# A two-layer graph network on Trainium2: which nodes of the output share a partition

## The chip, the cores and the metric

The kernel runs on one core of one Trainium2 chip. The metric is the device time of one execution in microseconds; the median of five runs of the kernel before is 2661.31 us. Five engines work side by side, each through its own list of instructions, and wait for one another by semaphores: TensorE (PE; its weight loads are listed apart as PEld), VectorE (DVE), ScalarE (ACT), GpSimd (POOL) and SyncE (SP). Data moves between the main memory (DRAM in the code) and the on-chip memory of 128 partitions through 16 DMA engines; SP and POOL put transfers on them, each through a queue of its own.

## What is computed

Sixteen graphs of N = 1024 nodes with C = 256 features go through two layers. All numbers are 32-bit floats. Cut to what matters:

```python
# layer 0: attention over the nodes, with a residual
h = relu(layernorm(x))
x = x + L0(h, para, adj, kv_w)
# layer 1: graph convolution and two linear layers, with a residual
h = relu(layernorm(x))
agg  = A_hat @ h                      # normalised adjacency, per graph
y1   = relu(batchnorm(agg @ W1.T + b1, g1, be1))    # 512 features
out  = batchnorm(y1 @ W2.T + b2, g2, be2)           # 256 features
x = x + out
```

The two batch norms take mean and variance over all nodes of all 16 graphs. So the second one can be applied only when the last graph's product with W2 is done, and the residual, the output of layer 0 (here x1), is needed again only then.

## The kernel before

P = 128 partitions, NT = N / P = 8 blocks of nodes, CC = C / P = 2 blocks of features, FB = 512.

**Layer 0 and the first half of layer 1** fill the span up to about 2380 us. `attention()` walks through the 16 graphs; the other products of the neighbouring graphs are woven between its steps by a hand-written order (`background`, `weave`, `advance`) in which every piece yields its cost in microseconds. Node t * 128 + p of a graph lies in partition p of the tile `xs[b]`, block t. When a graph's attention is complete, `normed` (for the last graph `normed_last`) puts the layer norm's output into a tile `h` and stores `xs[b]`, which is x1, from POOL's queue to `x1_d[b]` in DRAM (L725, L736). `x1_d[b]` has the shape [128, 8, 256], the same as the tile, so each partition's 8 KB are one contiguous run. POOL's queue also carries the stores of layer 1's hidden rows (`y_d`, L709), the sums of attention (`sums_d`, L919) and their return (`inv`, L924). SP's queue carries the loads.

**The second half of layer 1** is the generator `second`. For each graph `graph(b)` makes the product with W2, by seven partial products m1 to m7 (`product`, L1180), in a form that has features in partitions: `y2[b][k]` is a tile [128 features, 1024 nodes] for each block k of features. Between the graphs `load_x1` brings x1 of the graphs back from `x1_d` into tiles `xo` (L1111), two loads of 512 KB for each graph, one for each half of the blocks. The buffers of xo are borrowed from tiles that are no longer used: the first three graphs have a pool of their own, the next ones take buffers of `yin` and of `both`, graphs 8 to 10 the `y2` tiles of graphs 0 to 2, and later ones the buffers again that earlier xo leave.

**The tail** is the last loop of `second`, over the 16 graphs. `scales` and `affs` give the scale and shift of the second batch norm. For each graph:

1. ACT applies scale and shift to `y2[b][k]` in place (L1303), 1024 nodes in one instruction; for graph 0 in two parts of 512 nodes, so that the first transposes can begin sooner.
2. PE transposes blocks of 128 features x 128 nodes into PSUM, so that nodes are in partitions (L1311): four transposes (two node blocks, two feature blocks) make one tile `pt`. The pool `ps` has four such tiles.
3. DVE adds `pt` to the residual `xo` in place (L1317), two node blocks at a time.
4. After half a graph, which is two such sums, POOL stores 512 KB to `out` (L1318).
5. After the graph, `load_x1` is called if graphs remain to be loaded; SP waits there for the buffer.

The loop issues all instructions in this order; each engine runs its own list in order. A transposed block t holds the nodes t * 128 to t * 128 + 127, so that partition p gets node t * 128 + p:

```python
nc.tensor.transpose(
    pt[:, j, k * P : (k + 1) * P],
    y2[b][k][:, t * P : (t + 1) * P],
    ident,
)
```

In `out` a partition's four rows of a half graph lie 128 KB apart, and each row is 1 KB.

A second copy of the program (`layers(True)`) runs only if the attention's sums leave a safe range; with these inputs it doesn't.

Of the kernel before, what the change touches and what calls it, by code (L numbers as in the profile page):

```python
# [10 lines left out]
F32 = mybir.dt.float32  # L11
# [6 lines left out]
P = 128  # L18
# [5 lines left out]
def gnn_two_layers_kernel(  # L24
# [12 lines left out]
    nc = tc.nc  # L37
    B, N, C = x.shape
    H1 = w1_t.shape[1]
    NT = N // P  # L40
# [3 lines left out]
    FB = 512  # L44
# [8 lines left out]
    dram = ctx.enter_context(tc.tile_pool(name="dram", bufs=1, space=DRAM))  # L53
# [9 lines left out]
    stats1 = const.tile([P, HC, B * NH, 6], F32, name="stats1")  # L63
    mv1 = const.tile([P, HC, 2], F32, name="mv1")

    x1_d = [dram.tile([P, NT, C], F32, name=f"x1_d{b}") for b in range(B)]


    aht_d = dram.tile([7, NP // 2, P, TH, FB], F32, name="aht_d")
# [14 lines left out]
    def layers(shifted):  # L84
# [23 lines left out]
        xs, hs, hts, ats, qs, ks, vs = {}, {}, {}, {}, {}, {}, {}  # L108
# [19 lines left out]
        def run(*parts):  # L128
            for part in parts:
                while advance(part) is not None:  # L130
                    pass
            while queue:
                queue.pop(0)()

        def weave(main, *sides):

            for i, cost in enumerate(main):
                for start, side in sides:
                    if i >= start:
                        cost += next(side, 0.0)  # L140
                yield cost
            for _, side in sides:
                yield from side
# [16 lines left out]
        def load_x(b):  # L160
            xs[b] = p3.tile([P, NT, C], F32, tag="x", name=f"x_{b}")
            for half in range(2):
                t = slice(half * NT // 2, (half + 1) * NT // 2)
                nc.sync.dma_start(
                    out=xs[b][:, t], in_=x[b].rearrange("(t p) c -> p t c", p=P)[:, t]
                )

        def load_adj(q, th, name):
            t = p3.tile([P, TH, FB], F32, tag="adj", name=name)
            nc.sync.dma_start(  # L170
                out=t,
                in_=adj[th * TH * P : (th + 1) * TH * P, q * FB : (q + 1) * FB].rearrange(
                    "(t p) m -> p t m", p=P
                ),
            )
            return t

        load_x(0)
        kvw = const.tile([P, CC, 2 * C], F32, tag="kvw", name=f"kvw_{kind}")
        nc.sync.dma_start(out=kvw, in_=kv_w.rearrange("(k p) j -> p k j", p=P))  # L180
        rows = big.tile([P, NH, NT], F32, name="rows")

        def columns_of(col, name):

            cbs = []
            for g in range(NT // 4):
                cb = py.tile([P, 4, P], F32, tag="y", name=f"cb_{name}_{g}")
                nc.vector.tensor_copy(
                    cb, col[:, 4 * g : 4 * g + 4].unsqueeze(2).to_broadcast([P, 4, P])
                )  # L190
                cbs.append(cb)
            return cbs
# [191 lines left out]
        def differences(b, cbs):  # L384

            cbcs[b] = p1.tile([P, N], F32, tag="cbc", name=f"cbc_{b}")
            broadcast_row(cbcs[b], cbs, f"c{b}")
            weighers[b] = weigh(b)
# [332 lines left out]
        def normed(b):  # L721
            while (b, NH - 1) not in complete:
                yield 0.1
            yield from Norm(b, False).all()
            nc.gpsimd.dma_start(out=x1_d[b], in_=xs[b])  # L725
            if b + 3 < B:
                load_x(b + 3)

        def normed_last():

            norm = Norm(B - 1, False)
            for half in range(NH):
                while (B - 1, half) not in complete:
                    yield 0.0
                yield from norm.half(half * NT // 2)
            nc.gpsimd.dma_start(out=x1_d[B - 1], in_=xs[B - 1])  # L736

        def prepare(b, products):

# [270 lines left out]
        with st:  # L1010
            if shifted:
                for b in range(B):
                    if b > 0:
                        load_x(b)
                    run(Norm(b, True).all())
                    differences(b, columns_of(csums[b], f"c{b}"))
                    for k in range(CC):
                        transposed(b, k)
                    run(islice(weighers[b], AHEAD))
                    run(weave(plain_queries(b), (0, weighers[b])))  # L1020
                    if b == 0:
                        run(degrees(), graph())
                        load_later()
                        broadcast_row(later["dbc"], columns_of(dinv, "deg"), "deg")
                    run(keys_values(b))
                    shifted_attention(b)
                    norm = Norm(b, False)
                    run(norm.all())
                    nc.gpsimd.dma_start(out=x1_d[b], in_=xs[b])
                    if b == B - 1:  # L1030
                        attn.close()
                        turns.append(second(kind))
                    run(aggregate(b), hidden(b))
            else:
                norm = Norm(0, True)
                norm.stats(0, 1)
                norm.scale(0, 2)
                for t in range(2, NT, 2):
                    norm.stats(t, t + 1)
                    norm.shift(t - 2, 2)  # L1040
                    norm.relu(t - 2, t - 1)
                    norm.scale(t, 2)
                norm.shift(NT - 2, 2)
                norm.relu(NT - 2, NT - 1)
                products = keys_values(0)

                for k in range(CC):
                    transposed(0, k, (0,))
                run(islice(products, 2))
                for k in range(CC):  # L1050
                    transposed(0, k, (1,))
                differences(0, columns_of(csums[0], "c0"))
                run(weave(products, (0, islice(weighers[0], AHEAD))))
                load_x(1)
                load_x(2)
                run(weave(plain_queries(0), (0, weighers[0]), (5, Norm(1, True).all())))
                attention()
                attn.close()
                turns.append(second(kind))
                run(aggregate(B - 1), hidden(B - 1))  # L1060
# [3 lines left out]
    def second(kind):  # L1064
# [30 lines left out]
        def load_x1():  # L1095


            b = len(xos)
            name = f"xo_{kind}_{b}"
            HT = NT // 2  # L1100
            if not 8 <= b < 11:
                pool, tag = ((xp, "xo"), (io, "yin"), (wp, "both"))[(b % 11 > 2) + (b % 11 > 6)]
                xo = pool.tile([P, NT, C], F32, tag=tag, name=name)
                halves = [xo[:, :HT, :], xo[:, HT:, :]]
            else:
                halves = [
                    yp.tile([P, HT, C], F32, tag=f"y2_{b - 8}_{i}", name=f"{name}_{i}")
                    for i in range(2)
                ]
            for i in range(2):  # L1110
                nc.sync.dma_start(out=halves[i], in_=x1_d[b][:, i * HT : (i + 1) * HT, :])  # L1111
            xos.append(halves)

        with st:
# [17 lines left out]
            ys, t1s, t2s, y2 = {}, {}, {}, []  # L1132
# [162 lines left out]
                load_x1()  # L1295
            for b in range(B):

                for part in range(2 if b == 0 else 1):
                    n = slice(part * FB, N if b > 0 else (part + 1) * FB)
                    for k in range(CC):  # L1300
                        s2, sh2 = affs[k][2]
                        y = y2[b][k][:, n]
                        nc.scalar.activation(y, y, AF.Identity, bias=sh2, scale=s2)  # L1303
                for half in range(2):
                    xo = xos[b][half]
                    for g in range(NT // 4):
                        pt = ps.tile([P, 2, C], F32, tag="pz", name=f"pt_{kind}_{b}_{half}_{g}")
                        for j in range(2):
                            t = half * NT // 2 + 2 * g + j
                            for k in range(CC):  # L1310
                                nc.tensor.transpose(  # L1311
                                    pt[:, j, k * P : (k + 1) * P],
                                    y2[b][k][:, t * P : (t + 1) * P],
                                    ident,
                                )
                        dst = xo[:, 2 * g : 2 * g + 2, :]
                        nc.vector.tensor_add(dst, pt, dst)  # L1317
                    nc.gpsimd.dma_start(  # L1318
                        out=out[b].rearrange("(h t p) c -> h p t c", h=2, p=P)[half], in_=xo
                    )  # L1320
                if len(xos) < B:
                    load_x1()
# [62 lines left out]
```

## Time and profile before

The profile is taken of one execution, whose own time is 2663.26 us; its span, from the first to the last instruction, is 2661.5 us.

| what | value |
|---|---|
| median of 5 runs, lowest, highest | 2661.31, 2659.73, 2661.97 us |
| profiled execution, its span | 2663.26, 2661.5 us |
| mean granted clock of TensorE | 0.987 of full speed |
| busy: PE, DVE, ACT, POOL | 97%, 65%, 50%, 21% of the span |
| x1_d stores (POOL): number, size, issue on POOL, to landing | 16, 1024 KB, 540 to 632 ns, 10.1 us |
| xo loads (SP): number, size, to landing (median) | 32, 512 KB, 8.5 us |
| out stores (POOL): number, size, issue on POOL, to landing (median) | 32, 512 KB, 758 ns, 12.9 us |
| last product with W2, first transpose, first and last issue of an out store | 2582, 2587.7, 2591.7, 2649.0 us |
| activations of the tail: 1024 nodes, 512 nodes | 30 of 1229 ns, 4 of 806 ns |

An instruction group is named by its line, engine and operation, then output <- inputs with their shapes. "Idle before" is the time in which the engine waited just ahead of the group, and the arrow names what ended that wait. "To landing" runs from the issue of a transfer to its completion. The DMA share is the mean busy share of the 16 DMA engines; it can come out slightly over 1 when packets overlap. The granted clock is that of TensorE: 1.00 is full speed, 0.50 half.

### The profile page before, as it was taken

The numbers are of one execution on the slowest core, as the hardware profiler recorded it, in microseconds if no ns is written. First come the engines' busy times: TensorE is split into PE (matmuls) and PEld (weight loads), VectorE is DVE, ScalarE is ACT, GpSimd is POOL, SyncE is SP. The second block draws the span as 40 slices with busy tenths as digits, with TensorE's granted clock in tenths as the row PEclk, the third lists the DMA queues.
The fourth block names the chain that finished last, engine by engine and source line by source line (L and its number), as shares of the span: only waits on it lengthen the run. The fifth ranks groups of instructions, "written<-read, shape, count | busy, mean of one in ns | idle before, by whom it ended". The sixth has DMA issues, their size and how long they took to land. (4 is left out here: it accounts for less than half of the span.)

```text
span 2661.5 us, 32181 instructions
## 1 busy us (share of the span) xinstructions
PE 2573.4 (97%) x11882; PEld 951.9 (36%) x11882; DVE 1743.0 (65%) x2768; ACT 1337.3 (50%) x1937; POOL 564.8 (21%) x648
## 2 busy tenths in 40 slices
PE   8959999999999999999999999999999999999995
PEld 3323333333333333333333333333333333334443
DVE  5638676666767575767667676757676675557675
ACT  5635463636455554536373644545463634335544
POOL 1461101111111111111111111111101111126653
PEclk9979999999999999999999999999999999999997
DMA  4451425252423324242424233241425233455559
GB/s 158 139 186 52 174 80 171 80 175 71 145 93 114 123 67 161 73 171 84 171 80 148 93 132 100 90 144 60 170 84 170 80 120 103 132 201 194 201 180 374
DMA packets 131686, 355.59 MB, mean 134 GB/s; under 512 B 17984, under 2 KB 34880, under 8 KB 125376
## 3 DMA queue, kind: packets, MB, share of 16 engines
q1 hardware_dynamic: 104768, 274.25, 30.1%
q0 software_dynamic: 26752, 79.20, 8.9%
q8 instruction: 96, 1.57, 0.2%
q14 instruction: 70, 0.57, 0.1%
HBM read 278.67 MB, written 74.71 MB: 133 GB/s over the span
## 5 line engine op out<-in xcount | busy, mean ns | idle before, releaser
L866 ACT ACTIVATE p<-sc 128x1024 f32<-128x1024 f32 x512 | 495.5, 1020 | 606.4 <-PE sc L858 605.6
L888 DVE TENSOR_TENSOR acc<-acc,p 128x1024 f32<-128x1024 f32 x384 | 471.6, 1228 | 132.0 <-ACT p L866 111.5
L858 PE MATMUL sc<-q,k 64*128 64x512 f32 x2048 | 508.8, 615 | 0.4 <-ACT p L866 0.4
L899 PE MATMUL o<-p,v 128*64 128x512 f32 x2048 | 496.7, 606 | 0.0
L158 PE MATMUL pg<-w,h_a 128*64 128x512 f32 x1600 | 358.1, 592 | 3.6 <-DVE q L575 1.9
L158 PE MATMUL pa<-aht,h_b 128*64 128x512 f32 x1536 | 343.5, 592 | 0.0
L858 PEld LDWEIGHTS sc<-q,k 64*128 64x128 f32 x2048 | 176.1, 186 | 320.3 <-issue 296.6
L919 POOL DMA_DIRECT2D sums_d<-row x64 | 37.6, 587 | 1032.3 <-ACT row L918 1032.3
L158 PE MATMUL py<-at,w 128*64 128x512 f32 x1024 | 230.4, 592 | 0.0
L899 PEld LDWEIGHTS o<-p,v 128*64 128x64 f32 x2048 | 124.5, 136 | 285.4 <-issue 284.6
L408 DVE SCALAR_TENSOR_TENSOR w<-w,adj 128x1024 f32<-128x1024 f32 x128 | 157.1, 1227 | 103.2 <-ACT w L429 99.2
L158 PEld LDWEIGHTS pg<-w,h_a 128*64 128x64 f32 x1600 | 115.5, 137 | 232.0 <-issue 212.8
L158 PEld LDWEIGHTS pa<-aht,h_b 128*64 128x64 f32 x1536 | 110.3, 137 | 213.3 <-issue 197.5
L708 ACT ACTIVATE y<-py,vec 128x512 f32<-128x512 f32 x128 | 87.6, 684 | 168.3 <-PE py L158 111.4
L421 ACT ACTIVATE w<-cbc,csum 128x512 f32<-128x512 f32 x256 | 170.1, 715 | 0.0
L885 DVE TENSOR_TENSOR acc<-p,p 128x1024 f32<-128x1024 f32 x64 | 78.4, 1226 | 109.4 <-ACT p L866 109.4
L709 POOL DMA_DIRECT2D y_d<-y x128 | 70.3, 549 | 316.5 <-ACT y L708 315.3
L429 ACT ACTIVATE w<-w 128x1024 f32<-128x1024 f32 x128 | 134.9, 1054 | 1.8
L483 DVE TENSOR_TENSOR w<-w,w 128x1024 f32<-128x1024 f32 x112 | 132.7, 1215 | 1.8 <-DVE w L408 0.5
L158 PE MATMUL pv<-kvw_f,ht 128*64 128x256 f32 x1024 | 120.9, 384 | 10.4 <-DVE q L575 6.8
L924 POOL DMA_DIRECT2D inv<-sums_d x128 | 98.4, 772 | 146.4 <-DMA sums_d<-row 109.8
L158 PEld LDWEIGHTS py<-at,w 128*64 128x64 f32 x1024 | 74.2, 137 | 145.2 <-issue 128.7
(155 smaller groups left out, 2869.8 us busy)
## 6 DMA issues: line engine op xcount, KB each, us to landing
aht<-aht_d SPq DMA_DIRECT2D x224, 512.0 KB, 6.2
adj<-in_adj_dram SPq DMA_DIRECT2D x128, 512.0 KB, 4.4
y_d<-y POOLq DMA_DIRECT2D x128, 256.0 KB, 2.6
yin_f<-y_d SPq DMA_DIRECT2D x32, 1024.0 KB, 6.4
x<-in_x_dram SPq DMA_DIRECT2D x32, 512.0 KB, 5.1
para<-in_para_dram SPq DMA_DIRECT2D x64, 256.0 KB, 3.9
x_d<-x POOLq DMA_DIRECT2D x16, 1024.0 KB, 10.1
xo_f<-x_d SPq DMA_DIRECT2D x32, 512.0 KB, 8.5
```

The lines of the kernel that those rows point to most:

```text
L158: nc.tensor.matmul(dst[r], left[:, r], right, start=start, stop=stop)
L408: nc.vector.scalar_tensor_tensor(w, w, 1.0, a, op0=ALU.add, op1=ALU.mult)
L421: nc.scalar.activation(w[:, t, :], cbc[:, q * FB : (q + 1) * FB], AF.Abs, bias=csum[:, th * TH + t : th * TH + t + 1], scale=-1.0,)
L429: nc.scalar.activation(made[i], made[i], AF.Tanh, scale=-0.5 / C)
L483: nc.vector.tensor_sub(block(i)[part], block(x)[part], block(y)[part])
L708: nc.scalar.activation(y, made, AF.Identity, bias=b1[:, j : j + 1])
L858: nc.tensor.matmul(sc[:, e, :], ks[b][k][r, m * P : (m + 1) * P], qs[b][k][r, f * FB : (f + 1) * FB], start=True, stop=True,)
L866: nc.scalar.activation(pr, sc, AF.Exp)
L885: nc.vector.tensor_add(self.acc, self.held, pr)
L888: nc.vector.tensor_add(self.acc, self.acc, pr)
L899: nc.tensor.matmul(self.o[r, :], vs[b][k][:, m, r], pr[:, e, :], start=(m == 0), stop=(m == NT - 1),)
L924: nc.gpsimd.dma_start(out=self.inv[:, :, e], in_=sums_d[u][e].rearrange("(j q) -> q j", q=P))
```

## The change

Partition p now holds the eight nodes 8p to 8p + 7 of the output in place of p, 128 + p, 256 + p and so on. Four places change together:

- `x1_d[b]` becomes a plain [1024, 256] array of rows. The store of x1 (`store_x1`) still takes the tile `xs[b]` with node t * 128 + p in partition p, so it writes 1024 rows of 1 KB.
- `load_x1` reads it back with nodes 8p + 4h to 8p + 4h + 3 in partition p for half h: 4 KB in one run, as before.
- The transposes take every eighth node of `y2[b][k]` (nodes t, t + 8, t + 16, ...) in place of 128 neighbours; the two parts of graph 0's activations follow the same order, with t = 0 to 3 and 4 to 7.
- The store of half a graph to `out` has 4 KB in one run for each partition.

The number of instructions, of transfers and of bytes is the same.

```diff
--- before.py
+++ after.py
@@ -63,7 +63,7 @@
     stats1 = const.tile([P, HC, B * NH, 6], F32, name="stats1")
     mv1 = const.tile([P, HC, 2], F32, name="mv1")
 
-    x1_d = [dram.tile([P, NT, C], F32, name=f"x1_d{b}") for b in range(B)]
+    x1_d = [dram.tile([N, C], F32, name=f"x1_d{b}") for b in range(B)]
 
 
     aht_d = dram.tile([7, NP // 2, P, TH, FB], F32, name="aht_d")
@@ -164,6 +164,9 @@
                 nc.sync.dma_start(
                     out=xs[b][:, t], in_=x[b].rearrange("(t p) c -> p t c", p=P)[:, t]
                 )
+
+        def store_x1(b):
+            nc.gpsimd.dma_start(out=x1_d[b].rearrange("(t p) c -> p t c", p=P), in_=xs[b])
 
         def load_adj(q, th, name):
             t = p3.tile([P, TH, FB], F32, tag="adj", name=name)
@@ -722,7 +725,7 @@
             while (b, NH - 1) not in complete:
                 yield 0.1
             yield from Norm(b, False).all()
-            nc.gpsimd.dma_start(out=x1_d[b], in_=xs[b])
+            store_x1(b)
             if b + 3 < B:
                 load_x(b + 3)
 
@@ -733,7 +736,7 @@
                 while (B - 1, half) not in complete:
                     yield 0.0
                 yield from norm.half(half * NT // 2)
-            nc.gpsimd.dma_start(out=x1_d[B - 1], in_=xs[B - 1])
+            store_x1(B - 1)
 
         def prepare(b, products):
 
@@ -1026,7 +1029,7 @@
                     shifted_attention(b)
                     norm = Norm(b, False)
                     run(norm.all())
-                    nc.gpsimd.dma_start(out=x1_d[b], in_=xs[b])
+                    store_x1(b)
                     if b == B - 1:
                         attn.close()
                         turns.append(second(kind))
@@ -1095,6 +1098,7 @@
         def load_x1():
 
 
+
             b = len(xos)
             name = f"xo_{kind}_{b}"
             HT = NT // 2
@@ -1108,7 +1112,10 @@
                     for i in range(2)
                 ]
             for i in range(2):
-                nc.sync.dma_start(out=halves[i], in_=x1_d[b][:, i * HT : (i + 1) * HT, :])
+                nc.sync.dma_start(
+                    out=halves[i],
+                    in_=x1_d[b].rearrange("(p h t) c -> h p t c", h=2, p=P)[i],
+                )
             xos.append(halves)
 
         with st:
@@ -1295,11 +1302,11 @@
                 load_x1()
             for b in range(B):
 
+                nodes = [y.rearrange("c (p t) -> c t p", t=NT) for y in y2[b]]
                 for part in range(2 if b == 0 else 1):
-                    n = slice(part * FB, N if b > 0 else (part + 1) * FB)
                     for k in range(CC):
                         s2, sh2 = affs[k][2]
-                        y = y2[b][k][:, n]
+                        y = nodes[k][:, part * NT // 2 : (part + 1) * NT // 2] if b == 0 else y2[b][k]
                         nc.scalar.activation(y, y, AF.Identity, bias=sh2, scale=s2)
                 for half in range(2):
                     xo = xos[b][half]
@@ -1310,13 +1317,13 @@
                             for k in range(CC):
                                 nc.tensor.transpose(
                                     pt[:, j, k * P : (k + 1) * P],
-                                    y2[b][k][:, t * P : (t + 1) * P],
+                                    nodes[k][:, t],
                                     ident,
                                 )
                         dst = xo[:, 2 * g : 2 * g + 2, :]
                         nc.vector.tensor_add(dst, pt, dst)
                     nc.gpsimd.dma_start(
-                        out=out[b].rearrange("(h t p) c -> h p t c", h=2, p=P)[half], in_=xo
+                        out=out[b].rearrange("(p h t) c -> h p t c", h=2, p=P)[half], in_=xo
                     )
                 if len(xos) < B:
                     load_x1()
```

## The prediction

> **What bounds the kernel now.** I read the page's chain of waits first, then the chain in order of time from 2400 us on, then the busy time of each engine in stretches of 2 to 4 us behind it, and last the groups of instructions of the tail. Until the last product of layer 1 the chain is TensorE alone; then it changes hands:
>
> ```profile
> 2522.27 56.86 PE m_f L1180 x132
> ...
> 2588.01 0.82 ACT y_f L1303
> ...
> 2588.87 3.67 PE pt_f L1311 x16
> ...
> 2595.00 52.91 DMA out_dram<-xo_f x4
> ```
>
> The columns are start, length and what ran. From 2595 us the end is set by the output's stores, and no engine stands in the chain. Apart from layer 0's stores of x1 the whole change lies in this tail, so what it is worth is read there:
>
> ```profile
> 2586.00:2590.00 4.00, 1.61 (x7) 1.31 (x8) 1.41 (x8) 2.81 (x4) 0.81 (x2) 0.54 1.00 408
> 2590.00:2592.00 2.00, 2.00 (x11) 2.00 (x11) 1.68 (x3) 2.00 (x3) 0.35 (x1) 0.50 0.08 29
> 2592.00:2594.00 2.00, 2.00 (x14) 1.59 (x13) 1.49 (x3) 2.00 (x3) 1.14 (x2) 0.71 0.28 100
> ...
> 2612.00:2616.00 4.00, 3.94 (x28) 2.77 (x27) 4.00 (x8) 4.00 (x4) 1.17 (x2) 1.00 1.03 416
> 2616.00:2620.00 4.00, 3.97 (x29) 2.81 (x28) 4.00 (x8) 4.00 (x5) 1.09 (x2) 1.00 1.02 411
> ...
> 2628.00:2632.00 4.00, 2.63 (x12) 1.86 (x10) 1.99 (x4) 0.00 (x0) 1.51 (x2) 0.50 1.03 415
> ...
> 2640.00:2644.00 4.00, 0.00 (x0) 0.00 (x0) 0.00 (x0) 0.00 (x0) 2.81 (x4) 0.50 1.03 401
> 2644.00:2648.00 4.00, 0.00 (x0) 0.00 (x0) 0.00 (x0) 0.00 (x0) 2.28 (x4) 0.50 1.02 399
> ```
>
> After the stretch stand PE, weight load, DVE, ACT and POOL busy, then the granted clock, the DMA share and GB/s. Three things are to be seen. The DMA engines are almost idle from 2590 to 2594 us (0.08 and 0.28), while the first graph is scaled and transposed; from 2594 until about 2657 they are full (1.02 to 1.03). While loads of xo and stores of out run together they move 410 to 416 GB/s; when only stores are left, from 2636 us on, 399 to 405. And DVE is done with its last sum at 2637 us, some 20 us ahead of the last store: PE, DVE and ACT have room behind a full queue of stores.
>
> **What the longer runs are worth.** A store of half a graph (512 KB) now has 512 runs of 1 KB in the output, and 128 of 4 KB after. The page's packets say that queue 0 does not move such runs singly:
>
> ```profile
> DMA packets 131686, 355.59 MB, mean 134 GB/s; under 512 B 17984, under 2 KB 34880, under 8 KB 125376
> ...
> q0 software_dynamic: 26752, 79.20, 8.9%
> ```
>
> 34880 - 17984 = 16896 packets have 512 B to 2 KB. The loads of x with their 1 KB rows are 32 x 512 = 16384, and w2 (512 rows of 1 KB) makes 16896: nothing is left for the 16384 rows of the output. They already travel joined. The trace's packet records agree: the stores of out are packets of 4096 bytes, of 165 ns where only stores run, against 159 ns for a 4096-byte packet of a load whose run really is 4 KB. So what is to be won is the gap between 401 GB/s (stores alone) and 414 (loads of 4 KB runs alone, in the 2 us from 2586): 21 us x (1 - 401/414) = 0.66 us; and in the mixed 32 us before, at 411 on average, 32 x (1 - 411/414) = 0.23 us. Together -0.9 us. Bounds: 0, if the stores' rate is that of writing and not of the runs; and -1.5 us if the whole 63 us, at 408 on average, went at 418, the best 2 us of the tail. I take -0.9.
>
> [...]
>
> POOL issues 32 stores of 758 ns each (L1318, 512 runs); one of 128 runs costs 549 ns (y_d, L709). Only the first lies ahead of idle DMA engines: -0.2 us, the others have a full queue before them (bounds -0.2 and 0). The loads of xo keep runs of 4 KB (a partition's four rows of a half lie side by side before and after) and cost 0.
>
> **What layer 0's x1_d stores lose.** Each of the 16 (1 MB) has 128 runs of 8 KB now and 1024 of 1 KB after. By the two rows just used a run costs (758 - 549)/(512 - 128) = 0.54 ns, so an issue goes from 620 ns to 549 + 896 x 0.54 = 1.03 us: 16 x 0.4 = 6.6 us more on POOL, which is busy for 21% of the span. Queued behind it on POOL are the next y_d store and the row of sums of attention (sums_d), which waits 1032 us in all for ACT; that wait is the cover, and SP's next load of x comes only as much later as the store lands. The transfer itself, at the stores' rate, takes 2.6 us in place of 2.5. If POOL's cover were gone each would push TensorE back by at most 0.4 us, 6.6 in all; at a busy share of 2 to 4 tenths of DMA and with PE at 99% I take 0.
>
> **What the eighth columns cost.** Two operands of the tail become strided: the weights of the 256 transposes (the trace names y_f as the loaded operand, ident as the moving one), and the four activations of graph 0, which go by halves of the nodes. Both then touch an element every 32 bytes. No instruction in the trace reads so, and the price has to be bounded.
>
> ```profile
> L1311 PE MATMUL pt_f<-ident,y_f 128*128 128x128 f32 x256 | 40.8, 306 | 10.6 <-ACT y_f L1303 5.8 <-DVE xo_f L1317 4.3
> L1317 DVE TENSOR_TENSOR xo_f<-pt_f,xo_f 128x512 f32<-128x512 f32 x64 | 39.4, 680 | 10.3 <-PE pt_f L1311 4.1 <-SPq L1346 3.7 <-DMA xo_f<-x_d 2.5
> L1311 PEld LDWEIGHTS pt_f<-ident,y_f 128*128 128x128 f32 x256 | 30.8, 153 | 21.1 <-ACT y_f L1303 8.7 <-DVE xo_f L1317 6.0 <-issue 3.4
> ```
>
> Between 2594 and 2621 us PE loads four of these in 0.42 us and then waits 0.18 us for DVE: 0.105 us for each transpose (call it the pitch), 0.6 us for the four that fill a bank. Lower bound of the new pitch: that same 0.105. Upper row: the transposes of graph 0 at half clock, 16 in 3.67 us, 0.23 each; beyond it lies only the product of both, strided and at half clock, 0.43.
>
> [...]
>
> [...] With pitch p, PE needs 256p for the tail, from 2588.9 us. Behind the last transpose stand DVE's sum (0.7), its semaphore (0.3), the quickest store from issue to landing (6.1) and 1.5 us from the last landing to the end: 8.6 us. PE ends last only if 2588.9 + 256p + 8.6 exceeds 2661.5, that is p > 0.25. At 0.21 its 54 us end at 2643, with a backlog of stores still before the DMA engines: a half graph gives 1.3 us of store every 1.7 us, and 16 loads of 1.27 us come on top.
>
> So below 0.25 only the start counts, where the DMA engines are idle. The activation of k = 1 (0.82 us, on the chain at 2588.01) goes from 806 ns at 512 elements to at most the 1228 ns of 1024 elements; behind the longer one for k = 0 it ends 0.5 us later. Bounds 0 and +0.5; I take +0.5, for the waits behind it are short. The first eight transposes already run at the half clock with 0.21 us each: 0 if clock and stride hide each other, 8 x 0.21 = 1.7 us more if they multiply; the middle is +0.85, no row being nearer to either. The second eight could add as much again (upper bound 3.4 for both), but the first store's 1.3 us then covers part of it.
>
> **Sum.** -0.9 - 0.2 + 0 + 0.5 + 0.85 = +0.25 us on the profiled execution, whose span is 2661.5 us and whose time is 2663.26, 1.95 us above the median of the runs, 2661.31. The median should then be 2661.6. Ends of the case: -1.5 - 0.2 = -1.7, and 0.5 + 3.4 = +3.9: 2659.6 to 2665.2.
>
> **The rivals.** 0.2% is 5.3 us, about what a measurement of this kernel can tell from no change.
>
> TensorE takes over the tail (the other side): the strided weight loads come below 40% of their present rate, p over 0.25, and from then on each 0.01 us costs 256 x 0.01 = 2.6 us; over 5.3 us from p = 0.27. At three times the pitch (0.32) it is 2588.9 + 81.9 + 8.6 = 2679.4, +18 us, 2679; at four times, or at twice with the half clock (0.43), 2588.9 + 110 + 8.6 = 2707.5, +46 us, 2707. For it speaks the clock: with eight transposes in each 2.5 us it fell to 0.50 after 2628 us and stayed there, and loads that starve the array might bring that about at once. Against it: 40% slack now, and at 28 transposes in 4 us the clock held 1.00.
>
> The start grows: four slow activations (4 x 0.42 = 1.7), both halves of graph 0 multiplied (3.4) and no gain from the runs: +5.1, and about 2667 with a next graph that waits for ACT too. For it: DMA idle for 4 us there already; against: needs all of them.
>
> Faster by over 0.2%: the 63 full microseconds would have to move at 408 x 63/57.7 = 445 GB/s; no stretch shows more than 420. Idle from 2576 to 2581 isn't touched.
>
> That the runs bring nothing, since the packets were joined before, lies inside the first case (its term 0 in place of -0.9, 2662.5).
>
> **How the numbers follow.** No measurable change 0.47, TensorE takes over 0.38, the longer start 0.10, faster 0.05. The time is that of the likeliest single case, 2661.6, its own range 2659.6 to 2665.2. As nearly half of the chance is slower, the range for 8 in 10 reaches up into the second case, past three times the pitch but short of four: 2659.5 to 2695. Faster 0.05, within 0.2% 0.47, slower 0.48 (0.38 + 0.10).
>
> **What would show it.** In the changed profile: the mean of the weight loads of pt_f (137 to 140 ns at full clock now) and the starts of four of them tell p; the DMA share from 2594 us on must stay at 1.0 to the end, and the stores alone must move about 414 GB/s; the first store's issue tells the start (2591.65 now); the x1_d issues should read about 1.0 us with PE's 99% unchanged before 2582. The prediction is wrong if the chain of waits ends in PE pt_f rather than in the stores, if the DMA share has holes after the first graph, or if the part before 2582 us grows.

## The result, and the profile after

The changed kernel takes 2666.7 us (median of 30 runs, 2661.66 to 2669.16) against 2661.21 us (50 runs of the kernel before, 2658.06 to 2663.74): 5.5 us more, a ratio of 1.0021 with a 95% interval of 1.0016 to 1.0026. The profiled execution is one of the shorter: 2664.45 us with a span of 2662.7, where that of before had 2663.26 and 2661.5. So the two profiles differ by 1.2 us and the medians by 5.5, and the first thing to settle is which part of an execution varies by itself.

The last product of layer 1 shows it, in the instructions of TensorE in order of time (start, length, what), first before, then after:

```profile
2580.67 1.88 PE L1180 MATMUL m_f<-t_f,w_f 128*128 128x512 f32 x4
```

```profile
2577.09 1.88 PE L1187 MATMUL m_f<-t_f,w_f 128*128 128x512 f32 x4
```

It ends at 2582.55 us before and at 2578.97 after, 3.6 us sooner, although nothing in the change makes layer 0 or the products shorter. The kernel before, profiled a second time, ended it at 2580.40; over all profiled executions here it lies between 2578.97 and 2583.35. That is the variation between executions; the times of the kernel before alone spread over 5.7 us. What the change does is read from this instant on: the tail lasts 78.9 us before (2661.47 - 2582.55; 78.5 in the second profile) and 83.7 us after (2662.65 - 2578.97), about 5 us more.

The chain in order of time, after, from the last activations on:

```profile
2583.27 7.18 ACT y_f L1310 x6
2590.45 0.04 issue
2590.50 3.48 PE pt_f L1318 x15
...
2602.16 42.01 DMA out_dram<-xo_f x3
2644.16 0.70 issue
2644.86 0.55 POOLq L1352
```

The activations stand in it with 7.18 us, six of them, where one of 0.82 us stood before. Then come the stores, as before. The stretches of the tail after (PE, weight load, DVE, ACT, POOL busy, granted clock, DMA share, GB/s):

```profile
2588.00:2590.00 2.00, 1.76 (x8) 1.57 (x8) 1.00 (x2) 2.00 (x3) 0.63 (x1) 0.50 0.11 47
2590.00:2592.00 2.00, 1.71 (x8) 1.50 (x8) 1.25 (x2) 2.00 (x3) 0.54 (x1) 0.50 1.22 307
2592.00:2594.00 2.00, 2.00 (x12) 2.00 (x11) 1.52 (x3) 2.00 (x3) 0.53 (x1) 0.50 0.63 82
...
2640.00:2644.00 4.00, 0.00 (x0) 0.00 (x0) 0.00 (x0) 0.00 (x0) 1.85 (x4) 0.50 1.02 413
2644.00:2648.00 4.00, 0.00 (x0) 0.00 (x0) 0.00 (x0) 0.00 (x0) 0.70 (x2) 0.50 1.02 416
2648.00:2652.00 4.00, 0.00 (x0) 0.00 (x0) 0.00 (x0) 0.00 (x0) 0.00 (x0) 0.50 1.03 422
2652.00:2656.00 4.00, 0.00 (x0) 0.00 (x0) 0.00 (x0) 0.00 (x0) 0.00 (x0) 0.50 0.22 88
2656.00:2660.00 4.00, 0.00 (x0) 0.00 (x0) 0.00 (x0) 0.00 (x0) 0.00 (x0) 0.50 0.00 0
```

Three things are to be seen. From 2586 us the DMA engines are poorly fed (a share of 0.11 to 0.63), but for the first store (1.22), up to 2594, which is 15 us after the last product (11 us before). The stores alone move 413 to 422 GB/s in place of 399 to 405. And above all, the DMA engines stop in the stretch from 2652 us, and the span ends only at 2662.7. In the trace's packet records the last packet of a store ends 75.7 us after the last product before (75.3 in the second profile), and 75.4 after: the data is out at the same time; the parts below put faster stores against a later start. From there to the end of the span it takes 3.2 us before and 8.3 us after.

What happens in that time is in no group of instructions, as it is not counted as busy. The lines of the source where the program ends show it. First before, two lines of the source, then after (engine, with q for its sequencer, number, then min, median and max in ns, first and last start in us):

```profile
L1346 POOLq INC_SWDGE_SEM  x1: 492/492/492, 2658.8 to 2658.8; - x1
...
L1381 POOLq DRAIN  x3: 40/107/1302, 2659.3 to 2661.2; - x3
```

```profile
L1353 POOLq INC_SWDGE_SEM  x1: 1507/1507/1507, 2654.8 to 2654.8; - x1
...
L1388 POOLq DRAIN  x3: 40/107/5463, 2656.4 to 2662.4; - x3
```

When the last store has landed (2658.70 us before, 2654.71 after), POOL executes an INC_SWDGE_SEM and then the first of three DRAINs (the one with the maximum), and the other engines wait for it at the end of the program: their last semaphore waits end just behind it, from 2660.8 us on before and from 2662.0 us on after. What the two instructions do inside, the trace does not say. The two take 0.49 + 1.30 = 1.79 us before and 1.51 + 5.46 = 6.97 us after, 5.18 us more. Call it the closing time.

The remaining lines that answer to those of before, the groups of the tail and the packets:

```profile
L1318 PEld LDWEIGHTS pt_f<-ident,y_f 128*128 128x128 f32 x256 | 37.0, 201 | 16.7 <-ACT y_f L1310 9.0 <-DVE xo_f L1324 2.6 <-ACTq L1353 1.1
L1310 ACT ACTIVATE y_f<-y_f,sm_f 128x1024 f32<-128x1024 f32 x30 | 34.1, 1226 | 0.0
L1325 POOL DMA_DIRECT2D out_dram<-xo_f x32 | 17.2, 536 | 44.4 <-DVE xo_f L1324 25.8 <-DMA out_dram<-xo_f 13.2 <-issue 4.8
L1310 ACT ACTIVATE y_f<-y_f,sm_f 128x512 f32<-128x512 f32 x4 | 4.9, 1302 | 13.8 <-DVE sm_f L1085 13.8
```

```profile
DMA packets 133734, 355.59 MB, mean 134 GB/s; under 512 B 17984, under 2 KB 34880, under 8 KB 129472
...
q0 software_dynamic: 28800, 79.20, 8.9%
```

The strided activations of 512 nodes take 1302 ns in place of 806, more than 1024 contiguous ones (1226). The strided weight loads have a median of 194 ns in place of 140. Queue 0 has 2048 packets more: the 2048 runs of 8 KB of x1_d were single packets, and the 16384 runs of 1 KB are now joined, four to a packet of 4 KB. The packets under 2 KB are the same to the last one: the 16384 rows of the output never were among them.

### The profile page after: what moved, and what is told of

It reads as the page before. It is cut to its first block, busy times and chain, and to the rows that moved or that the text cites. A ratio compares the mean times of both kernels' runs of the same rounds, so it can differ in the third digit from the quotient of the medians.

```text
span 2662.7 us, 32181 instructions
## 1 busy us (share of the span) xinstructions
PE 2575.1 (97%) x11882; PEld 958.2 (36%) x11882; DVE 1743.1 (65%) x2768; ACT 1338.5 (50%) x1937; POOL 563.6 (21%) x648
## 2 busy tenths in 40 slices
DMA packets 133734, 355.59 MB, mean 134 GB/s; under 512 B 17984, under 2 KB 34880, under 8 KB 129472
## 4 chain that ended last, share of the span: by engine, by line
PE 86%; DVE 5%; POOL 3%; DMA 3%; ACT 1%; issue 1%; SPq 0%; POOLq 0%; DVEq 0%
PE sc L861 17%; PE o L902 16%; PE pa L158 14%; PE pg L158 11%; PE py L158 8%; PE m_f L1187 7%; PE pk L158 4%; PE pv L158 2%; PE sums L919 2%; DMA out_dram<-xo_f 2%; DVE acc L891 1%; PE htp L382 1%; PE ot L937 1%; DVE q L514 1%; POOL lnsm_b L82 1%
## 5 line engine op out<-in xcount | busy, mean ns | idle before, releaser
L891 DVE TENSOR_TENSOR acc<-acc,p 128x1024 f32<-128x1024 f32 x384 | 471.6, 1228 | 131.8 <-ACT p L869 111.3
```

What stands on the lines that cost most here:

```text
L891: nc.vector.tensor_add(self.acc, self.acc, pr)
```

## The experiments: the change in its parts

The change was taken apart, each part alone in the kernel before. A part alone leaves the rows of the output, or the residual, in another order than the reference, so these kernels serve for their times only. The kernel before itself was run again beside them, as a measure of chance:

> The kernel before, unchanged, as the measure of what two equal kernels differ by and of how its closing instructions on POOL vary from one profiled execution to the next. Theory E (the changed kernel loses its time behind the last store, in POOL's closing INC_SWDGE_SEM and DRAIN, which took 0.49 + 1.30 us in the profile of before and 1.51 + 5.46 us in that of the changed kernel, and this belongs to the kernel): again 1.8 us in all, give or take 0.5, ratio 1.000 within 0.0005. Rival C (the closing time is chance and the loss lies elsewhere): anything from 1.8 to 7 us.

Measured: 2661.28 us against 2661.15, ratio 1.000 (0.9991 to 1.0009); closing 0.49 + 1.30 us, to the nanosecond as in the first profile. Two equal kernels cannot be told apart here below about 0.09%, 2.4 us, and the closing time is not a matter of chance.

**Only the stores of out (e_stores).**

```diff
-                        out=out[b].rearrange("(h t p) c -> h p t c", h=2, p=P)[half], in_=xo
+                        out=out[b].rearrange("(p h t) c -> h p t c", h=2, p=P)[half], in_=xo
```

> Only the stores of out take the new form (128 runs of 4 KB); x1_d, the activations and the transposes stay, so the rows of the output come out in another order. Theory E with the stores' form as its cause: the last store lands 1 to 1.5 us sooner (stores alone at 416 in place of 401 GB/s), the closing time grows from 1.8 to about 7 us, in sum +3.5 to +4.5 us. Theory R (the cause is x1_d's store of 1024 runs) and theory S (the strided reads): closing 1.8 us and -1 to -1.5 us in all.

Measured: 2664.26 us against 2661.15, ratio 1.0011 (1.0001 to 1.002), +3.1 us. The last packet ends 74.7 us after the last product, 0.6 to 1.0 us sooner than in the two profiles of the kernel before. The stores alone:

```profile
2640.00:2644.00 4.00, 0.00 (x0) 0.00 (x0) 0.00 (x0) 0.00 (x0) 1.69 (x4) 0.50 1.03 414
2644.00:2648.00 4.00, 0.00 (x0) 0.00 (x0) 0.00 (x0) 0.00 (x0) 1.50 (x3) 0.50 1.03 419
```

and the closing:

```profile
L1346 POOLq INC_SWDGE_SEM  x1: 1167/1167/1167, 2657.0 to 2657.0; - x1
...
L1381 POOLq DRAIN  x3: 40/107/4075, 2658.2 to 2662.8; - x3
```

5.24 us, 3.45 more than before. So the part of the change that was meant to help does make the stores faster, and loses the gain, and some 2.5 us on top, after the last byte is out.

**Only x1_d as rows (e_rows).**

```diff
-    x1_d = [dram.tile([P, NT, C], F32, name=f"x1_d{b}") for b in range(B)]
+    x1_d = [dram.tile([N, C], F32, name=f"x1_d{b}") for b in range(B)]
...
-            nc.gpsimd.dma_start(out=x1_d[b], in_=xs[b])
+            nc.gpsimd.dma_start(out=x1_d[b].rearrange("(t p) c -> p t c", p=P), in_=xs[b])
...
-                nc.sync.dma_start(out=halves[i], in_=x1_d[b][:, i * HT : (i + 1) * HT, :])
+                nc.sync.dma_start(
+                    out=halves[i],
+                    in_=x1_d[b].rearrange("(p h t) c -> h p t c", h=2, p=P)[i],
+                )
```

> Only x1_d changes: stored as 1024 runs of 1 KB, loaded with nodes 8p to 8p + 7 in partition p; transposes and stores of out stay, so the residual is added to other nodes. Theory R: POOL's longer issues (0.98 in place of 0.62 us) or what they leave in its queue bring the loss, +3 to +5.5 us, or a closing time of about 7 us. Theory E with the stores' form as its cause, and theory S: 0 to +0.5 us, closing 1.8 us.

Measured: 2662.39 us against 2661.15, ratio 1.0004 (0.9995 to 1.0014), not to be told from no change; the last packet at 75.4 us as before, the closing 0.71 + 2.20 = 2.91 us, 1.1 more:

```profile
L1384 POOLq DRAIN  x3: 40/107/2201, 2656.3 to 2659.0; - x3
```

That surprised both theories: the last store of x1_d is issued some 300 us ahead of the end, and yet the closing remembers it. The form of out's stores alone can't be the cause. Its median lies 1.2 us higher, about what the closing adds, so that no gain or loss of layer 0 is to be seen.

**Only the strided reads (e_cols).**

```diff
+                nodes = [y.rearrange("c (p t) -> c t p", t=NT) for y in y2[b]]
...
-                        y = y2[b][k][:, n]
+                        y = nodes[k][:, part * NT // 2 : (part + 1) * NT // 2] if b == 0 else y2[b][k]
...
-                                    y2[b][k][:, t * P : (t + 1) * P],
+                                    nodes[k][:, t],
```

> Only the reads change: transposes take every eighth column, the activations of graph 0 go by halves of the nodes; x1_d and the stores of out stay, so nodes stand in other rows. Theory S (strided reads delay the first stores and the DMA engines stay idle longer): first store 0.5 us later after the last product, the full stretch of the DMA engines about 3 us later, +2 to +4 us, closing 1.8 us. Theory E: 0 to +1.5 us from the start alone, closing 1.8 us.

Measured: 2662.38 us against 2661.15, ratio 1.0006 (0.9997 to 1.0015). The first store goes out 9.64 us after the last product (9.10 before), the third 13.75 (12.44, and 12.78 in the second profile), the last packet ends at 76.9 us; the closing is 1.79 us. Five profiles with the tail of before (two of the kernel before, and d_b1, d_b2 and d_b_small below) end the last packet at 75.3 to 76.05, so it is 0.8 to 1.6 us late. A price of about 1.2 us is likely, but the interval of the medians holds zero.

The three parts add up: +3.1, +1.2 and +1.2 us make 5.6, against 5.5 for the whole; as each has an interval of some 2.4 us to either side, part of this agreement is luck. The closing times alone make 3.45 + 1.12 = 4.6 against 5.18.

To see whether the start's price is that of the activations or of the weight loads, the activations of graph 0 were made contiguous (shown against e_cols):

```diff
-                for part in range(2 if b == 0 else 1):
-                    for k in range(CC):
-                        s2, sh2 = affs[k][2]
-                        y = nodes[k][:, part * NT // 2 : (part + 1) * NT // 2] if b == 0 else y2[b][k]
-                        nc.scalar.activation(y, y, AF.Identity, bias=sh2, scale=s2)
+                for k in range(CC):
+                    s2, sh2 = affs[k][2]
+                    y = y2[b][k]
+                    nc.scalar.activation(y, y, AF.Identity, bias=sh2, scale=s2)
```

> The strided transposes alone (as e_cols), but the activations of graph 0 over 1024 nodes, contiguous. Strided reads cost 1.2 us in e_cols. If the strided activations are the cause (1302 in place of 806 ns, four of them ahead of graph 1): second and third store at 11.2 and 12.9 us after the last product in place of 11.9 and 13.8, and 0 to +0.5 us in all. If the strided weight loads are: still +1.2 us, although the second and third store go out sooner.

Measured: 2662.41 us against 2661.34, ratio 1.0003 (0.9993 to 1.0012). The second and third store go out at 11.2 and 12.7 us, as foreseen for the activations, but the last packet ends at 76.2 us, between e_cols and the kernel before. Two kernels whose tail is that of before, d_b2 and d_b_small below, also ended it at 76.05. So 0.7 us of the last packet is chance, and this one is inconclusive: which of the two strided reads costs more stays open.

## The experiments: what the closing time follows

The kernel before with one and with two more transfers on POOL's queue at the very start of the program (the edit with two is shown; these kernels and the two with small transfers ran once each, for the trace):

```diff
     nc.gpsimd.memset(ones, 1.0)
+    for _ in range(2):
+        nc.gpsimd.dma_start(
+            out=seen.rearrange("p a (t c) -> p (a t) c", c=16),
+            in_=x[0].rearrange("(t p) c -> p t c", p=P)[:, :, :16],
+        )
```

> The kernel before with one more transfer on POOL's queue at the very start, of 1024 runs of 64 B into a tile that is overwritten later. Theory P (the closing time follows a position in POOL's queue that every run moves, wherever in the program it is issued): closing between 1.8 and 7 us, some 4. Theory F (only the form of the stores of out and x1_d counts): 1.8 us.

> The same with two such transfers, 2048 runs more than the kernel before, which is also the changed kernel's surplus (16 x 896 more for x1_d, 32 x 384 fewer for out). Theory P: closing about 7 us, as in the changed kernel. Theory F: 1.8 us.

Measured: 0.49 + 1.30 us with one, 0.58 + 1.63 us with two. Neither theory holds. It isn't the position that 2048 runs would give (7 us); but it isn't the form of out's and x1_d's stores alone either: one transfer at the start changes nothing, but two, 2.6 ms ahead of the end, move it by 0.41 us.

The numbers themselves gave the next theory. All DRAINs seen were 1302 ns plus a whole multiple of 81.6 ns: 0 (before, e_cols, d_b1), 4 (d_b2: 1629), 11 (e_rows: 2201), 34 (e_stores: 4075), 35 (f_a_sp below: 4157), 51 (after: 5463). The INC_SWDGE_SEMs were 492 ns plus the same multiple of some 20 ns. And between after and f_a_sp, which takes 16 stores off POOL, lie 16 steps. So a step looks like one transfer: POOL would walk, at the end, through the transfers that its queue still keeps on its books, and transfers of few runs leave room for more of them. That says what eight small transfers must do, issued in layer 1 ahead of all stores of out:

```diff
                 graph(b, ahead_of(b + 1))
+                if kind == "f" and 4 <= b < 8:
+                    for i in (2 * b, 2 * b + 1):
+                        nc.gpsimd.dma_start(out=sums_d[i][:, :HD], in_=ones[0:2, :])
```

> The changed kernel with eight more transfers on POOL, of two runs of 256 B each, between the products of graphs 4 to 7 of layer 1, ahead of all stores of out. So far the closing DRAIN was 1302 ns plus a whole multiple of 81.6 ns (0, 4, 11, 34, 35, 51 times), and INC_SWDGE_SEM 492 plus the same multiple of 20 ns; taking 16 stores from POOL took 16 steps off. Theory N (one step for each POOL transfer that POOL's queue still keeps on its books; transfers of few runs leave room for more of them): 59 steps, DRAIN 5463 + 8 x 82 = 6.1 us and INC 1.67 us, a step or two fewer if they push out older ones. Theory P (position, by runs: 16 runs more): unchanged, 5.46 and 1.51 us.

> The same eight transfers in the kernel before, whose 32 stores of 512 runs each follow. Theory N: these stores push the small ones off the books, closing 1.30 and 0.49 us as before, or a few steps more. If the number of POOL transfers alone counted, 8 steps more: 1.95 and 0.65 us.

Measured in the changed kernel:

```profile
L1356 POOLq INC_SWDGE_SEM  x1: 1667/1667/1667, 2654.7 to 2654.7; - x1
...
L1391 POOLq DRAIN  x3: 40/107/6117, 2656.4 to 2663.1; - x3
```

59 steps, eight more, in both instructions (6117 - 5463 = 654 = 8 x 81.75 and 1667 - 1507 = 160 = 8 x 20). In the kernel before, whose 32 stores of 512 runs follow:

```profile
L1349 POOLq INC_SWDGE_SEM  x1: 492/492/492, 2657.5 to 2657.5; - x1
...
L1384 POOLq DRAIN  x3: 40/107/1302, 2658.0 to 2659.9; - x3
```

no step at all. Both are as the theory of the books has it, and neither the run count nor the transfer count alone gives both. One step for each transfer late in the program is shown in the changed kernel; that a step is a record which POOL's queue keeps, pushed out by later transfers with many runs, is a reading, not something that the trace shows directly. The reading asks that a store of 128 runs take less room than one of 512, which is the author's estimate and which no run here shows; POOL's issue is shorter for it too, 536 ns against 758.

How many transfers are kept stays open, and books from which each new transfer pushes the oldest can't be the whole of it. The last 32 stores of e_rows are those of the kernel before, with more runs ahead of them, and yet it has 11 steps more; the changed kernel has more runs than e_stores, and 51 steps against 34. Books that fill up and are then cleared of many records at once are a rival that allows both, since the count then depends on where the last clearing fell. No run here was made to test it. So the rule of the steps stays open.

## The experiments: the closing time out of the way

If the closing is the loss, it has to vanish when POOL can close while stores still run. SP has no load left after graph 7's turn, so it can issue the stores of graphs 8 to 15:

```diff
-                    nc.gpsimd.dma_start(
+                    (nc.sync if b >= B // 2 else nc.gpsimd).dma_start(
                         out=out[b].rearrange("(p h t) c -> h p t c", h=2, p=P)[half], in_=xo
                     )
```

> The changed kernel with the stores of out of graphs 8 to 15 issued by SP, which has no load left by then; POOL's last store is that of graph 7. Theory E (the loss is POOL's closing time behind the last landing, 6.97 us in the changed kernel): POOL closes while the stores of SP still run, and the end follows the last landing by some 1.5 us in place of 8.3: about 6 us less than the changed kernel, that is 1 to 2 us less than the kernel before (2659.5 to 2660.5 where that is 2661.2). Rival S (the stores themselves are late): the same time as the changed kernel within 1 us. Rival: runs issued by SP go by another route and are slower, then the stretch of stores alone shows under 400 GB/s and less is won.

Measured: 2659.96 us against 2661.27, ratio 0.9997 (0.9988 to 1.0006).

```profile
L1353 POOLq INC_SWDGE_SEM  x1: 1187/1187/1187, 2635.0 to 2635.0; - x1
...
L1388 POOLq DRAIN  x3: 40/107/4157, 2636.2 to 2657.5; - x3
```

The closing still takes 5.34 us, but it starts at 2635 us and is over at 2640.4, while the DMA engines still have 15 us of stores before them:

```profile
2644.00:2648.00 4.00, 0.00 (x0) 0.00 (x0) 0.00 (x0) 0.00 (x0) 0.00 (x0) 0.50 1.01 412
2648.00:2652.00 4.00, 0.00 (x0) 0.00 (x0) 0.00 (x0) 0.00 (x0) 0.00 (x0) 0.50 1.03 421
2652.00:2656.00 4.00, 0.00 (x0) 0.00 (x0) 0.00 (x0) 0.00 (x0) 0.00 (x0) 0.50 0.34 139
```

The last packet ends 75.4 us after the last product, as in the changed kernel, and the end follows 2.7 us later in place of 8.3. So the loss goes away with the closing, while the data ends at the same time. With the same stores, the same strided reads and the same x1_d, the median is 6.7 us below the 2666.7 of the changed kernel; the kernel before lies at 2661.2 to 2661.3 in both comparisons. Against the kernel before the difference of 1.3 us is within chance.

With the contiguous activations of graph 0 added (the edit of e_cols_whole):

> As f_a_sp, and the activations of graph 0 go over 1024 nodes at once, which is contiguous: 2 of 1.23 us in place of 4 of 1.30. If the strided activations are what delays the first stores (theory S for the 1.2 us that the strided reads cost alone), the second and third store go out 1 to 2 us sooner and the time falls by another 1 to 1.4 us. If the strided weight loads (194 in place of 140 ns) are the cause, by 0.2 us at most.

Measured: 2660.75 us against 2661.27, ratio 0.9997 (0.9988 to 1.0006). The second and third store went out at 11.2 and 12.9 us in place of 11.9 and 13.8, and the last packet ended at 75.8, no sooner. The expected 1 to 1.4 us did not come; like e_cols_whole this does not settle the start.

Last, whether the run's length matters when SP issues: the kernel before, with its runs of 1 KB, and the same edit.

> The kernel before with the stores of out of graphs 8 to 15 issued by SP, in runs of 1 KB. If SP's queue moves runs singly (packets of 1024 bytes take 46 ns in the trace of before, the loads of x, so 4 KB take 184 ns against 165 joined), the 16 stores take 16 x 8 x 19 ns = 2.4 us longer and the end's gain is 0.5 us: +2 us against the kernel before, and 16 x 512 = 8192 packets more under 2 KB on the page. If SP joins them too: -0.5 us.

Measured: 2661.86 us against 2661.34, ratio 1.0002 (0.9992 to 1.0012); the last packet at 76.8 us, 0.8 to 1.5 later than in the five profiles with the tail of before, the end 2.7 us behind it. The stores alone and the packets:

```profile
2644.00:2648.00 4.00, 0.00 (x0) 0.00 (x0) 0.00 (x0) 0.00 (x0) 0.00 (x0) 0.50 1.09 382
```

```profile
DMA packets 137831, 355.60 MB, mean 134 GB/s; under 512 B 17984, under 2 KB 43072, under 8 KB 131520
```

43072 - 34880 = 8192 packets more under 2 KB: SP's queue sends each 1 KB run by itself, at 382 GB/s, where POOL's joins four and reaches 401. The 2.4 us came out as 0.8 to 1.5. POOL's closing, off the path here, is 0.85 + 2.77 us:

```profile
L1381 POOLq DRAIN  x3: 40/107/2772, 2638.0 to 2661.6; - x3
```

That is 18 steps in place of 0 although 16 transfers were taken away; these were the ones of many runs, so the books allow it, but they did not foretell the 18. In the stretch of stores alone, runs of 4 KB are worth 3% on POOL's queue (401 to 414) and 9% on SP's (382 to 416).

## Why the prediction was right or wrong

The median of 2666.7 us lies in the stated range, and 1.5 us above the likeliest case's own (to 2665.2). It lies there by luck: the range reached up to 2695 for the case in which TensorE takes over the tail, and that did not happen. The likeliest case, no change beyond 0.2%, lies at its border: the ratio's interval is 1.0016 to 1.0026, a small loss but a loss. The mechanism that decided is in none of the cases.

- **The step that failed** is the "1.5 us from the last landing to the end". The prediction took it from the one profile at hand and used it as a constant in the price of TensorE's rival, and left it out of the sum as unchanged. Even in that profile it was longer: the last store landed at 2658.70 us, 2.77 us ahead of the end. In the changed kernel it is 7.94 us. It holds POOL's closing, which grew from 1.79 to 6.97 us: +5.18 us of the 5.5. The row was there to be read in the profile of before, a DRAIN of 1302 ns behind the last landing; since it isn't counted as busy, no group of instructions has it. That it would grow with this change could not be read from one trace.
- **The stores' gain**, -0.9 us by the gap between 401 and 414 GB/s: right in size, though 0.7 us of the last packet is chance. Alone they brought it 0.6 to 1.0 us forward, at 414 to 419. Two rows were misread on the way: the 408 GB/s hold from 2600 us on and not from 2594 (252, 334 and 358 GB/s in the three stretches of 2 us before that), and the best 2 us had 420, not 418. Neither moves the sum. That queue 0 joins its runs, read from the packet counts, is borne out by the count that didn't move.
- **POOL's issues**: 0.55 us foreseen for an out store, 0.54 measured; 1.03 for x1_d, 0.97 measured. That layer 0 hides the latter: right as far as can be seen, the last product isn't later; but x1_d's runs came back in the closing, +1.1 us, where no one looked.
- **The start**: the first store was 0.54 us later, 0.5 taken for the activation; that an activation of 512 elements would take at most the 1228 ns of 1024 was wrong, the strided ones took 1302. The 0.85 for the first transposes, the middle of none and a doubling by the stride that no run shows, did not come: the eight took 1.97 us, 0.13 more than half of the 3.67 for sixteen before. But the price went on in the second part: four activations of 1.30 us in a row, so the second store was 1.2 and the third 1.9 us later. The sum said +1.35 for both, e_cols gave about +1.2 with an interval that holds zero: near in size, but not from where it was expected.
- **The strided operands** are slower: 1302 against 806 ns on ACT, a median of 194 against 140 ns on the weight loads. Yet TensorE did not take over the tail: from the fourth on the next stores went out every 1.20 us, as before, the clock held 1.00 from 2596 to 2624 us, and the DMA engines stayed full from there to the end of the data (1.00 to 1.04). The slack that was shown in the profile covered it, as said.
- **The longer start**, called at about 2667 us, has the measured time and not its cause: it asked for +5.1 us before the stores, and the last packet was not late at all, 75.4 us after the last product against 75.3 and 75.7.

## What to carry to other kernels

Follow the chain past the last byte: what stands between the last landing and the end is part of the time (2.77 us before, 7.94 after), and sequencer instructions such as a DRAIN aren't in the busy groups. With the last transfers on POOL's queue its closing lay on the path, 1.79 us before and 6.97 after; giving the last ones to SP's queue let POOL close early and took 6.7 us off the changed kernel. There long runs pay (416 against 382 GB/s where stores run alone), since in these traces that queue doesn't join short ones: with runs of 1 KB the same edit won nothing on the kernel before (2661.86 against 2661.34 us), and none of the kernels here is faster than that one beyond chance. Where two executions differ ahead of the change, measure from an instant behind the variation and ahead of the edit.

## What the runs showed that was not expected

- POOL's closing takes 1.79 us and 102 ns more (82 in DRAIN, 20 in INC_SWDGE_SEM) for each of 4 to 59 steps, to the nanosecond the same in the two profiles of the kernel before. In the changed kernel 16 transfers fewer and 8 more change it by 16 and 8 steps; in the kernel before 16 fewer add 18 steps and 8 more change nothing.
- Fewer runs in the last transfers made the closing longer: 34 steps more for stores of 128 runs in place of 512.
- The instant of the last product varied by 4.4 us between profiled executions of programs that are the same up to there or nearly so (2578.97 to 2583.35), much more than anything in the tail but the closing.
